# Windowed attention beside a binary FFN on one core: six visits a sequence in place of nine, 64-row scores in one pass, one rotation of seven PSUM banks

## The chip, the cores and the metric

The kernel runs on one core of a Trainium2 chip. The metric is the device time of one execution in microseconds (us), the lower the better. TensorE (PE in the profile) multiplies matrices and loads its weights (PEld), VectorE is DVE, ScalarE is ACT, GpSimd is POOL and SyncE is SP, which here issues nearly all DMAs. PSUM, where matmuls leave their results, is used here as eight banks; one bank holds 512 float32 numbers in each of 128 partitions.

## The reference

There are 8 sequences of 512 rows of 256 numbers. For each sequence, `x + attention(LN(x)) * silu(ffn(LN(x)))`:

```python
# attention: 16 heads of 16 numbers, q and k rotated (RoPE)
q, k, v = split(xn @ in_proj_w.T)
delta = pos[:, None] - pos[None, :]
mask = (delta >= 0) & (delta < 250)
scores = einsum('bhtd,bhsd->bhts', q, k) * 16 ** -0.5
attn = softmax(where(mask, scores, -huge))
s = einsum('bhts,bhsd->bhtd', attn, v) @ out_proj_w.T
# FFN: weights are +1 or -1, widths 512 (xn, -xn) -> 1024 -> 1024 -> 256
h = relu(s0 * [xn, -xn] @ W0) * 2;  h = relu(s1 * h @ W1) * 2;  h = s2 * h @ W2
out = x + s * silu(h)
```

## The kernel before, in words

Activations lie transposed: features in the partitions, the 512 positions of a sequence along the free dimension. Numbers that need float32 accuracy are held as two parts, high and low. In the FFN the high part is float16 and the low part fp32r. A tile of the second hidden layer (`layer`, "h2", 128 features) takes 16 matmuls of 512 columns; its bank is then read twice, by `high` (ACT, L535, relu) and by `low` (DVE, L533, what is left over). The third layer, `last` ("z"), takes 16 more. The first layer ("h1") takes 4 a tile.

**q and k.** `project` (L394) gives two halves of q and two of k; DVE multiplies them by cosines and sines (`times`, L410), POOL adds these up (`rotate`, L431), ACT copies out the high part (`split_hi`, L448: the tiles `kh` and `qh`) and DVE subtracts for the low part (`split_lo`, L455). `to_dram` writes high and low into DRAM, and `stack` (L458 to L464) loads them again, head by head: a head has 32 rows in the partitions, 16 of its high part and 16 of its low part, so four heads fill a tile. A score is k times q in full, that is high by high, low by low, high by low and low by high. With 32 rows that takes two matmuls that add up in PSUM ("turns"): k against q with its parts in order (`q0`), then against q with its parts exchanged (`q1`). Four heads are a group, and there are four groups.

**A visit.** Attention is cut into blocks: of a group g, the 128 keys j, and the queries that see them (378, 378, 256 and 128 for the four j). `steps` puts the 16 blocks, three of them cut in two, into nine visits a sequence of up to 512 columns a head. A visit (`step`, L860) first puts the score matmuls on PE (`scores`, L752), then the matmuls of the visit before with v (`values`, L826), then two ACT instructions of 2 banks each for the exponentials (`exponentials`, L771), then the masks on POOL (`mask`, L787 and L794: affine selects that put zeros outside the window). The sums over a row come out of the values matmul as an extra column. Between visits PE works on FFN layers and projections. After a group is done, `keep` copies V and the sums S out of the bank of `values` (even groups on ACT L850 and L851, odd groups on DVE L844 and L845).

**PSUM.** Before, three pools share the eight banks: `ps_s`, two tiles of two banks each, for scores; `ps_o`, one bank, for the values; `ps_m`, a rotation of three banks, for everything else (h, z, v, q, k and the output projection `att_ps`).

**The gate.** `z` is scaled (DVE, L616) and later turned into silu by `gate_ready`: exponential on ACT (L643), plus one on POOL (L647), two reciprocals of 256 columns on DVE (L652), and a product on POOL (L654). `project_o` (L959) multiplies attention by the output weights into a bank (`att_ps`); `product` (DVE, L981) multiplies bank and gate, and frees the bank; `store` adds x on POOL (L988) and writes out. This runs for two halves (u = 0 and 1) a sequence. The gate and output of sequence b are made late in sequence b+1, beside its last visits.

**Order.** Each engine works its instructions off in the order in which they were issued. That order comes from a small planner (`run`): a heap of pieces of work, each with a planned time (42 planner units a sequence) and a cost; a piece may return follow-ups with a delay (exponentials after scores, masks after exponentials). `attention` (L868) places the visits between FFN pieces. So an instruction that waits holds up whatever was put behind it on its engine.

The steps of the prediction touch `to_dram`, `stack`, `steps`, `scores`, `exponentials`, `mask`, `values`, `step`, `layer`, `gate_ready`, `project_o` and `divide`.

## Time and profile before

| what | value |
|---|---|
| median of 3 runs | 606.43 us (605.62 to 607.2) |
| the profiled execution | 605.76 us |
| its span, from the first to the last instruction | 603.9 us |
| outside the span | 1.86 us |
| PE busy | 593.9 us, 98% of the span |
| DVE, ACT, POOL busy | 337.3, 289.7 and 280.6 us |
| clock granted to PE | 1.00 |
| DMA | 75.52 MB, 125 GB/s on average |

Reading it: a group of instructions has its line, engine, operation and tiles, then its busy time and the mean of one; behind the bar stands the idle time of the engine just before these instructions, and what ended it. The chain that ended last is followed back from the last instruction. Busy time of PE includes pipelined matmuls, so 98% does not say that PE runs at its peak; it says that it seldom stands still. Where starts are compared below, they are of one kind of instruction, since modelled ends of matmuls overlap.

### The profile page before, as it was taken

Reading aid. Unit: us, or ns where it says so; the run is one execution under the profiler, and the core shown is the slowest. Engines: PE = TensorE matmul, PEld = TensorE weight load, DVE = VectorE, ACT = ScalarE, POOL = GpSimd, SP = SyncE. Lnnn points to the kernel's source line nnn. Section 1 sums busy time; section 2 is a strip of 40 time slices with the busy share of each in tenths; the row PEclk is TensorE's granted clock in tenths of the full one; section 3 lists DMA queues with packets and bytes.
Section 4 is the critical chain, followed back from the end, with each engine's and each line's share of the span. In section 5 each row is a group of like instructions: output and inputs, shape, how many; then the busy total and the mean of one; then the engine's idle time right before and its main releaser. Section 6 shows DMA issues by size and latency. Waiting matters only on the chain.

```text
span 603.9 us, 11263 instructions
## 1 busy us (share of the span) xinstructions
PE 593.9 (98%) x4492; PEld 366.7 (61%) x4492; DVE 337.3 (56%) x578; ACT 289.7 (48%) x411; POOL 280.6 (46%) x346
## 2 busy tenths in 40 slices
PE   7999999999999999999999999999999999999996
PEld 5654666555665556556566566655665556667785
DVE  6854535557456474655736656466565555635456
ACT  4755664444553535545354454543545425554432
POOL 2745522366423653437524456144662256436433
PEclk9999999999999999999999999999999999999999
DMA  8652642227331353415433254242442315322102
GB/s 269 235 177 88 231 144 90 87 82 237 108 125 53 133 186 107 126 53 203 118 107 125 82 198 131 88 130 99 174 163 88 109 71 210 112 56 71 58 15 64
DMA packets 43177, 75.52 MB, mean 125 GB/s; under 512 B 10224, under 2 KB 17904, under 8 KB 43120
## 3 DMA queue, kind: packets, MB, share of 16 engines
q1 hardware_dynamic: 40688, 72.53, 35.7%
q10 hardware_dynamic: 2432, 2.23, 1.2%
q8 instruction: 36, 0.59, 0.4%
q14 instruction: 21, 0.17, 0.1%
HBM read 44.83 MB, written 29.91 MB: 124 GB/s over the span
## 4 chain that ended last, share of the span: by engine, by line
PE 92%; DMA 3%; DVE 2%; POOL 1%; issue 0%; ACT 0%; ACTq 0%; SPq 0%; DVEq 0%
PE h_ps L524 46%; PE po L826 12%; PE z_ps L578 9%; PE sc L752 9%; PE v_ps L371 4%; PE att_ps L959 4%; PE ka_ps L394 2%; PE qa_ps L394 2%; PE kb_ps L394 2%; PE qb_ps L394 2%; DMA q<-dq 1%; DMA wqkv_sb<-in_w_qkv_dram 1%; DMA dq<-m_qa 1%; POOL m_qa L431 1%; POOL m_ka L431 0%
## 5 line engine op out<-in xcount | busy, mean ns | idle before, releaser
L771 ACT ACTIVATE p<-sc 128x1024 f32<-128x1024 f32 (+2 forms) x144 | 138.3, 1013 | 77.2 <-PE sc L752 46.8
L524 PE MATMUL h_ps<-h1l,w_sb 128*128 128x512 f32 (+1 forms) x576 | 146.1, 395 | 0.0
L787 POOL TENSOR_SCALAR_AFFINE_SELECT p<-p 128x512 f32<-128x512 f32 x128 | 93.7, 738 | 101.9 <-ACT p L771 101.1
L524 PE MATMUL h_ps<-h1h,w_sb 128*128 128x512 f16 (+1 forms) x576 | 123.1, 357 | 0.0
L524 PEld LDWEIGHTS h_ps<-h1l,w_sb 128*128 128x128 f32 x576 | 100.2, 188 | 29.5 <-issue 9.2
L524 PEld LDWEIGHTS <-w_sb 128*128 128x128 f16 x704 | 61.2, 98 | 74.7 <-issue 29.2
L535 ACT ACTIVATE h2h<-h_ps 128x512 f16<-128x512 f32 (+1 forms) x72 | 39.5, 548 | 124.5 <-PE h_ps L524 124.5
L794 POOL TENSOR_SCALAR_AFFINE_SELECT p<-p 128x512 f32<-128x512 f32 (+1 forms) x96 | 51.7, 539 | 87.7 <-ACT p L771 81.5
L826 PE MATMUL po<-p,v_pad 128*32 128x378 f32 (+4 forms) x1216 | 76.6, 372 | 0.0
L533 DVE SCALAR_TENSOR_TENSOR h2l<-h_ps,h2h 128x512 fp32r<-128x512 f32 (+1 forms) x72 | 44.0, 611 | 46.0 <-ACT h2h L535 45.9
L533 DVE SCALAR_TENSOR_TENSOR h1l<-h_ps,h1h 128x512 fp32r<-128x512 f32 x64 | 43.4, 688 | 42.2 <-ACT h1h L535 41.2
L652 DVE RECIPROCAL den<-den 128x256 f32<-128x256 f32 (+1 forms) x32 | 52.4, 1643 | 22.2 <-POOL den L647 22.2
L752 PEld LDWEIGHTS sc<-q,k 32*128 32x128 f32 x1216 | 44.2, 184 | 30.5 <-issue 22.5
L752 PE MATMUL sc<-q,k 32*128 32x378 f32 (+4 forms) x1216 | 58.0, 307 | 0.8 <-DMA q<-dq 0.8
L524 PE MATMUL h_ps<-xl,w_sb 128*128 128x512 f32 x128 | 52.3, 489 | 0.0
L826 PEld LDWEIGHTS po<-p,v_pad 128*32 128x32 f32 x1216 | 31.7, 109 | 28.4 <-issue 17.0
L535 ACT ACTIVATE h1h<-h_ps 128x512 f16<-128x512 f32 x64 | 38.1, 597 | 19.0 <-PE h_ps L524 19.0
L949 POOL TENSOR_TENSOR V<-V,R 128x512 f32<-128x512 f32 x16 | 20.6, 1286 | 46.3 <-DVE R L948 41.4
L524 PE MATMUL h_ps<-xh,w_sb 128*128 128x512 f16 x128 | 38.4, 382 | 0.1
L578 PE MATMUL z_ps<-h2l,w_sb 128*128 128x512 f32 (+1 forms) x144 | 35.7, 390 | 0.0
L431 POOL TENSOR_TENSOR m_ka<-m_ka,m_kb 128x512 f32<-128x512 f32 x16 | 20.1, 1274 | 31.7 <-DVE m_kb L410 31.7
L616 DVE TENSOR_SCALAR gate<-z_ps,scales 128x512 f32<-128x512 f32 (+1 forms) x16 | 11.5, 718 | 38.4 <-PE z_ps L578 38.4
(102 smaller groups left out, 679.1 us busy)
## 6 DMA issues: line engine op xcount, KB each, us to landing
q<-dq SPq DMA_DIRECT2D x64, 256.0 KB
dq<-qh SPq DMA_DIRECT2D x16, 512.0 KB
dq<-m_qa SPq DMA_DIRECT2D x16, 512.0 KB
k<-dk SPq DMA_DIRECT2D x32, 256.0 KB
dk<-kh SPq DMA_DIRECT2D x8, 512.0 KB
dk<-m_ka SPq DMA_DIRECT2D x8, 512.0 KB
x<-in_x_dram SPq DMA_DIRECT2D x30, 128.0 KB
xT<-in_x_t_dram SPq DMA_DIRECT2D x7, 512.0 KB
```

The lines of the kernel that those rows point to most:

```text
L394: nc.tensor.matmul(ps[:, cols], wqkv_sb[:, c, ds(col, P)], st["xT"][:, c, cols], start=(c == 0), stop=(c == EC - 1),)
L431: nc.gpsimd.tensor_tensor(m[:, i], m[:, i], n[:, i], op)
L524: nc.tensor.matmul(ph, weights(w, p, c, ts(f, P)), st[src + p][:, c, cols], start=(k == 0), stop=(k == n - 1),)
L533: nc.vector.scalar_tensor_tensor(lo, ph, 0.0, hi, ALU.max, ALU.subtract)
L535: high = lambda: nc.scalar.activation(hi, ph, AF.Relu)
L578: nc.tensor.matmul(pz, weights(w2, p, c, ts(f, P)), st["h2" + p][:, c, cols], start=(c == 0 and p == "h"), stop=(c == NF1 - 1 and p == "l"),)
L652: nc.vector.reciprocal(part, part)
L752: nc.tensor.matmul(sc[r // 2][:, r % 2, ds(off, n)], st["k0", g][row, ts(j, P)], st[f"q{turn}", g][row, ds(j * P + first, n)], start=(turn ...
L771: nc.scalar.activation(p[:, 2 * half : 2 * half + 2, :n], sc[half][:, :, :n], AF.Exp, scale=D ** -0.5,)
L787: nc.gpsimd.affine_select(out=block, in_=block, compare_op=ALU.is_ge, fill=0.0, base=0, pattern=[[0, 4], [1, P]], channel_multiplier=-1,)
L794: nc.gpsimd.affine_select(out=block, in_=block, compare_op=ALU.is_ge, fill=0.0, base=-1, pattern=[[0, 4], [-1, beyond]], channel_multiplier=1,
L826: nc.tensor.matmul(po[32 * r : 32 * r + 32, ds(j * P + first, n)], v_columns(j, g, r), p_[:, r, ds(off, n)], start=(j == 0), stop=(done an ...
```

## The change

The change does the same arithmetic with other shapes and another use of PSUM.

- A head's q and k get 64 rows: k as high, low, high, low and q as high, low, low, high. One matmul then holds all four products. A tile holds two heads, so a group has two pairs of tiles. Each of k's and q's parts is written to DRAM twice.
- Six visits a sequence (two blocks cut in two), each with up to 512 columns a head in four banks (x) and up to 256 in two more (y, two heads in a bank): up to 768 columns.
- All PSUM but the bank of `values` becomes one rotation of seven one-bank tiles (`ps_b`), from which scores, h, z, v, q, k and `att_ps` all take theirs.
- Exponentials are one instruction for each bank, six a visit; masks come in three parts, each behind two of the exponentials.
- Probabilities lie in tiles of two banks' width, eight in the pool. `S` and `R` share three buffers.
- The planner's cost of a visit is 2.5 in place of 1.7, and its exponentials may be issued up to 1.4 units before the values.

```diff
-    probs = ctx.enter_context(tc.tile_pool(name="probs", bufs=2))
+    probs = ctx.enter_context(tc.tile_pool(name="probs", bufs=8))
-    ps_s = ctx.enter_context(tc.tile_pool(name="ps_s", bufs=2, space=PSUM))
     ps_o = ctx.enter_context(tc.tile_pool(name="ps_o", bufs=1, space=PSUM))
-    ps_m = ctx.enter_context(tc.tile_pool(name="ps_m", bufs=3, space=PSUM))
+    ps_b = ctx.enter_context(tc.tile_pool(name="ps_b", bufs=7, space=PSUM))
+    def bank(name):
+        return ps_b.tile([P, T], F32, tag="b", name=name)
...
-            st["h"] = ps_m.tile([P, T], F32, tag="mm", name=f"h_ps_{b}_{f}")
+            st["h"] = bank(f"h_ps_{b}_{f}")
...
-        pp = ps_m.tile([P, T], F32, tag="mm", name=f"att_ps_{b}_{u}")
+        pp = bank(f"att_ps_{b}_{u}")
...
-        for turn in range(2 if what == "q" else 1):
-            if part == 0:
-                st["dram", what, turn] = dram.tile(
-                    [P, 4, T], F32, tag=f"{what}{turn}", name=f"d{what}{turn}_{b}"
-                )
+        if part == 0:
+            st["dram", what] = dram.tile([P, 8, T], F32, tag=what, name=f"d{what}_{b}")
+        for turn in range(2):
+            place = 2 * turn + (part ^ (turn if what == "q" else 0))
             nc.sync.dma_start(
-                st["dram", what, turn][:, ds(2 * (part ^ turn), 2), :], tile_.bitcast(F32)
+                st["dram", what][:, ds(2 * place, 2), :], tile_.bitcast(F32)
             )
...
-        for what in ("k0", "q0", "q1"):
-            t = stacks.tile([P, T], F32R, tag=what, name=f"{what}_{b}_{g}")
-            rows = st["dram", what[0], int(what[1])][32 * g : 32 * g + 32]
-            nc.sync.dma_start(t.bitcast(F32), rows.rearrange("p n t -> (p n) t"))
-            st[what, g] = t
+        for pair in range(2):
+            for what in "kq":
+                t = stacks.tile([P, T], F32R, tag=f"{what}{pair}", name=f"{what}_{b}_{g}_{pair}")
+                rows = st["dram", what][ds(32 * g + 16 * pair, 16)]
+                nc.sync.dma_start(t.bitcast(F32), rows.rearrange("p n t -> (p n) t"))
+                st[what, g, pair] = t
...
-            dp, dv = 1.5, 1.0
+            dp, dv = 1.5, 0.85
...
+    HALF_BANK = T // 2
+    steps = []
+    for g in range(0, NG, 2):
+        for of_x, of_y in (
+            ([(g, *whole_0), (g, *whole_3)], (g, *whole_2)),
+            ([(g, *whole_1), (g + 1, *whole_3)], (g + 1, *whole_2)),
+            ([(g + 1, *whole_0), (g + 1, *left_1)], (g + 1, *right_1)),
+        ):
+            blocks, off = [], 0
+            for block in of_x:
+                blocks.append((*block, 0, off))
+                off += block[3]
+            assert off <= T and of_y[3] <= HALF_BANK
+            steps.append(blocks + [(*of_y, 1, 0)])
...
     def scores(b, i):
         st = states[b]
+        sc = [bank(f"sc_{b}_{i}_{k}") for k in range(6)]
+        for y in range(2):
+            for pair in range(2):
+                for g, j, first, n, y_, off in steps[i]:
+                    if y_ != y:
+                        continue
+                    for r in range(2):
+                        row = slice(64 * r, 64 * r + 64)
+                        at = off + HALF_BANK * pair if y else off
+                        nc.tensor.matmul(
+                            sc[r + (4 if y else 2 * pair)][:, ds(at, n)],
+                            st["k", g, pair][row, ts(j, P)],
+                            st["q", g, pair][row, ds(j * P + first, n)],
+                            start=True,
+                            stop=True,
+                            skip_group_check=True,
+                        )
+        return sc
+
+    def exponentials(b, i, sc):
+        tiles = [
+            probs.tile([P, 2, T], F32, tag="p", name=f"p_{b}_{i}_{k}") for k in range(3)
         ]
+        n = sum(x[3] for x in steps[i] if not x[4])
+        n_y = steps[i][-1][3]
+
+        def of_bank(k):
+            p, s_ = tiles[k // 2][:, k % 2], sc[k]
+            if k < 4:
+                p, s_ = p[:, :n], s_[:, :n]
+            elif n_y < HALF_BANK:
+                p, s_ = (
+                    a.rearrange("p (u n) -> p u n", u=2)[:, :, :n_y] for a in (p, s_)
+                )
+            nc.scalar.activation(p, s_, AF.Exp, scale=D ** -0.5)
+            out = [(0.6, jobs[k + 1])] if k < 5 else []
+            if k % 2:
+                out.append((0.6, masks[k // 2]))
+            return out
...
-        S = st["S", g] = outs.tile([P, T], F32, tag=f"S{odd}", name=f"S_{b}_{g}", bufs=2)
+        S = st["S", g] = outs.tile([P, T], F32, tag="S", name=f"S_{b}_{g}", bufs=3)
...
-        return [(-0.7 if had else 0.0, exps)] + more
+        tiles, exps, rest = exponentials(b, i, sc)
+        pending.append((rest, (b, i, tiles)))
+        return [(-1.4 if had else 0.0, exps)] + more
...
-            out.append((times[n], 1.7, lambda n=n: step(b, n)))
+            out.append((times[n], 2.5, lambda n=n: step(b, n)))
...
-        R = outs.tile([P, T], F32, tag="R", name=f"R_{b}_{pair}")
+        R = outs.tile([P, T], F32, tag="S", name=f"R_{b}_{pair}", bufs=3)
```

More of the change, by code (lines that the diff above doesn't have):

```diff
@@ L331, in turn_x @@
                     st["x" + p] = one.tile([P, EC, T], dt, tag="x" + p, name=f"x{p}_{b}")
-        if not plain and t == 2:
-            pt = ps_o.tile([P, T], F32, tag="po", name=f"xnT_ps_{b}_{t}")
-            pt = pt[:, : EC * P].rearrange("p (c q) -> p c q", c=EC)
-        elif not plain and t < 2:
-            pt = ps_s.tile([P, 2, T], F32, tag="sc", name=f"xnT_ps_{b}_{t}")
-            pt = pt[:, 0, : EC * P].rearrange("p (c q) -> p c q", c=EC)
-        else:
-            pt = ps_m.tile([P, EC, P], F32, tag="mm", name=f"xnT_ps_{b}_{t}")
+        pt = bank(f"xnT_ps_{b}_{t}")[:, : EC * P].rearrange("p (c q) -> p c q", c=EC)
         for c in range(EC):
@@ L364, in project_v @@
         st = states[b]
-        if b == 0:
-            v = ps_s.tile([P, 2, T], F32, tag="sc", name=f"v_ps_{b}_{t}")[:, 0, :E]
-            v = v.rearrange("p (n s d) -> p n s d", s=2, d=D)
-        else:
-            v = ps_m.tile([P, H // 2, 2, D], F32, tag="mm", name=f"v_ps_{b}_{t}")
+        v = bank(f"v_ps_{b}_{t}")[:, :E].rearrange("p (n s d) -> p n s d", s=2, d=D)
         for c in range(EC):
@@ L384, in project @@
         col = E * "qk".index(what) + P * "ab".index(part)
-        if b == 0 and what == "q":
-            ps = ps_s.tile([P, 2, T], F32, tag="sc", name=f"{what}{part}_ps_{b}")[:, 0]
-        elif half == 1:
+        if half == 1:
             ps = st.pop(part)
         else:
-            ps = ps_m.tile([P, T], F32, tag="mm", name=f"{what}{part}_ps_{b}")
-            st[part] = ps
+            ps = st[part] = bank(f"{what}{part}_ps_{b}")
         for cols in [slice(0, T)] if half is None else [ts(half, T // 2)]:
@@ L562, in last @@
         f, cols = outputs(b)[u]
-        if how == "final":
-            pz = ps_s.tile([P, 2, T], F32, tag="sc", name=f"z_ps_{b}_{u}")[:, 0, : T // 2]
-        else:
-            pz = ps_m.tile([P, T], F32, tag="mm", name=f"z_ps_{b}_{u}")
-            if b + 1 == B:
-                pz = pz[:, : T // 2]
+        pz = bank(f"z_ps_{b}_{u}")
+        if b + 1 == B:
+            pz = pz[:, : T // 2]
         if how == "at once":
@@ L630, in plain_ffn @@
             for f in range(NF0):
-                ps = ps_m.tile([P, T], F32, tag="mm", name=f"f_h_{b}_{f}")
+                ps = bank(f"f_h_{b}_{f}")
                 for c in range(n):
@@ L721, in tile_attention_times_gated_ffn @@
     left_1, right_1 = (1, 0, cut), (1, cut, seen[1] - cut)
-    steps = [
-        [(0, *whole_0), (0, *left_1)],
-        [(0, *right_1), (0, *whole_2)],
-        [(0, *whole_3), (1, *whole_0)],
-        [(1, *whole_1), (1, *whole_3)],
-        [(1, *whole_2), (2, *whole_2)],
-        [(2, *whole_0), (2, *left_1)],
-        [(2, *right_1), (2, *whole_3), (3, *whole_3)],
-        [(3, *whole_0), (3, *left_1)],
-        [(3, *right_1), (3, *whole_2)],
-    ]
+    HALF_BANK = T // 2
[12 more added lines that the diff above has]
+            steps.append(blocks + [(*of_y, 1, 0)])
     used = [[n for n, step_ in enumerate(steps) if g in {x[0] for x in step_}] for g in range(NG)]
@@ L739, in once, with place @@
         return lambda: calls.pop()() if calls else None
+    def place(tiles, r, y, off, n):
+        if y:
+            return tiles[2][:, r % 2, ds(HALF_BANK * (r // 2) + off, n)]
+        return tiles[r // 2][:, r % 2, ds(off, n)]
     def scores(b, i):
         st = states[b]
-        sc = [
-            ps_s.tile([P, 2, T], F32, tag="sc", name=f"sc_{b}_{i}_{half}")
-            for half in range(2)
-        ]
-        off = 0
-        for g, j, first, n in steps[i]:
-            for turn in range(2):
-                for r in range(4):
-                    row = slice(32 * r, 32 * r + 32)
-                    nc.tensor.matmul(
-                        sc[r // 2][:, r % 2, ds(off, n)],
-                        st["k0", g][row, ts(j, P)],
-                        st[f"q{turn}", g][row, ds(j * P + first, n)],
-                        start=(turn == 0),
-                        stop=(turn == 1),
-                        skip_group_check=True,
-                    )
-            off += n
@@ L761, in scores @@
-        return sc, off
-    def exponentials(b, i, sc, n):
-        p = probs.tile([P, 4, T], F32, tag="p", name=f"p_{b}_{i}")
-        def exps():
-            half_of(0)
-            return [(0.3, second)]
-        def half_of(half):
-            nc.scalar.activation(
-                p[:, 2 * half : 2 * half + 2, :n], sc[half][:, :, :n], AF.Exp,
-                scale=D ** -0.5,
-            )
-        second = once(lambda: half_of(1) or [(0.6, masks)])
-        masks = once(lambda: mask(i, p))
-        return p, lambda: (second(), masks()), once(exps)
@@ L780, in mask @@
-    def mask(i, p):
-        off = 0
-        for g, j, first, n in steps[i]:
+        sc = [bank(f"sc_{b}_{i}_{k}") for k in range(6)]
[15 more added lines that the diff above has]
+                        )
@@ new lines, in scores @@
+        return sc
+    def exponentials(b, i, sc):
+        tiles = [
+            probs.tile([P, 2, T], F32, tag="p", name=f"p_{b}_{i}_{k}") for k in range(3)
+        ]
+        n = sum(x[3] for x in steps[i] if not x[4])
[13 more added lines that the diff above has]
+            return out
+        jobs = [once(lambda k=k: of_bank(k)) for k in range(6)]
+        masks = [once(lambda k=k: mask(i, tiles, k)) for k in range(3)]
+        return tiles, jobs[0], lambda: [f() for f in jobs + masks]
@@ L785, in mask @@
+    def mask(i, tiles, k):
+        p, heads = tiles[k], 2
+        if k == 2:
+            p, heads = p.rearrange("p a (u n) -> p (a u) n", u=2), 4
+        for g, j, first, n, y, off in steps[i]:
+            if y != k // 2:
+                continue
             if first == 0:
@@ L788, in mask @@
                     out=block, in_=block, compare_op=ALU.is_ge, fill=0.0,
-                    base=0, pattern=[[0, 4], [1, P]], channel_multiplier=-1,
+                    base=0, pattern=[[0, heads], [1, P]], channel_multiplier=-1,
                 )
@@ L795, in mask @@
                     out=block, in_=block, compare_op=ALU.is_ge,
-                    fill=0.0, base=-1, pattern=[[0, 4], [-1, beyond]],
+                    fill=0.0, base=-1, pattern=[[0, heads], [-1, beyond]],
                     channel_multiplier=1,
                 )
-            off += n
     def v_columns(j, g, r):
@@ L805, in tile_attention_times_gated_ffn, with values @@
     over = []
-    def values(b, i, p):
+    def values(b, i, tiles):
         st = states[b]
-        blocks, off = [], 0
-        for g, j, first, n in steps[i]:
-            blocks.append((g, j, first, n, p, off))
-            off += n
+        blocks = [(*x[:4], tiles, *x[4:]) for x in steps[i]]
         g = over[0][0] if over else blocks[0][0]
@@ L817, in values @@
         now.sort(key=lambda x: x[1:3] != (0, 0))
+        if not now:
+            return
         over[:] = [x for x in blocks if x[0] != g]
@@ L823, in values @@
         done = i >= used[g][-1]
-        for k, (_, j, first, n, p_, off) in enumerate(now):
+        for k, (_, j, first, n, tiles_, y, off) in enumerate(now):
             for r in range(4):
@@ L828, in values @@
                     v_columns(j, g, r),
-                    p_[:, r, ds(off, n)],
+                    place(tiles_, r, y, off, n),
                     start=(j == 0),
@@ L854, in flush @@
         if pending:
-            *before, of_step = pending.pop()
-            for f in before:
-                f()
+            before, of_step = pending.pop()
+            before()
             return values(*of_step)
     def step(b, i):
-        sc, n = scores(b, i)
+        sc = scores(b, i)
         had = len(pending)
         more = flush() or []
-        p, masks, exps = exponentials(b, i, sc, n)
-        pending.append((exps, masks, (b, i, p)))
-        return [(-0.7 if had else 0.0, exps)] + more
+        tiles, exps, rest = exponentials(b, i, sc)
+        pending.append((rest, (b, i, tiles)))
+        return [(-1.4 if had else 0.0, exps)] + more
     def attention(b, among):
@@ L1019, in add_up @@
     def add_up():
-        total = ps_m.tile([1, 3 * B], F32, tag="mm", name="total")
+        total = bank("total")[0:1, : 3 * B]
         nc.tensor.matmul(total, ones[:, 0:1], counts, start=True, stop=True)
@@ L1077, in shifted @@
         st = states[b]
-        row = slice(32 * r, 32 * r + 32)
+        row = slice(64 * (r % 2), 64 * (r % 2) + 64)
         j0 = max(0, t - 2)
@@ L1081, in shifted @@
         h = 4 * g + r
-        sc = ps_s.tile([P, 2, T], F32, tag="sc", name=f"f_sc_{b}_{t}_{h}")
-        for turn in range(2):
-            nc.tensor.matmul(
-                sc[:, 0, :n],
-                st[f"q{turn}", g][row, ts(t, P)],
-                st["k0", g][row, ds(j0 * P, n)],
-                start=(turn == 0),
-                stop=(turn == 1),
-            )
-        p = probs.tile([P, 4, WIN], F32, tag="p", name=f"f_p_{b}_{t}_{h}")
-        x_, e, eT = p[:, 0, :n], p[:, 1, :n], p[:, 2, :]
-        nc.scalar.copy(x_, sc[:, 0, :n])
+        sc = bank(f"f_sc_{b}_{t}_{h}")[:, :n]
+        nc.tensor.matmul(
+            sc,
+            st["q", g, r // 2][row, ts(t, P)],
+            st["k", g, r // 2][row, ds(j0 * P, n)],
+            start=True,
+            stop=True,
+        )
+        p, turned_ = (
+            probs.tile([P, 2, T], F32, tag="p", name=f"f_p{k}_{b}_{t}_{h}") for k in range(2)
+        )
+        x_, e, eT = p[:, 0, :n], p[:, 1, :n], turned_[:, 0, :WIN]
+        nc.scalar.copy(x_, sc)
         off = (t - j0) * P
@@ L1107, in shifted @@
         nc.scalar.activation(e, x_, AF.Exp, scale=D ** -0.5)
-        pt = ps_s.tile([P, 2, T], F32, tag="sc", name=f"f_pt_{b}_{t}_{h}")
+        pt = bank(f"f_pt_{b}_{t}_{h}")
         for j in range(n // P):
-            nc.tensor.transpose(pt[:, 0, ts(j, P)], e[:, ts(j, P)], ident)
-        nc.scalar.copy(eT[:, :n], pt[:, 0, :n])
+            nc.tensor.transpose(pt[:, ts(j, P)], e[:, ts(j, P)], ident)
+        nc.scalar.copy(eT[:, :n], pt[:, :n])
         for j in range(n // P):
```

## The prediction

> **What bounds the kernel now.** I read the page first, then the chain of waits in order of time for one steady sequence, then the timelines of DVE and POOL where the gate is made, then each engine's waits. The page:

> ```profile
> span 603.9 us, 11263 instructions
> ...
> PE 593.9 (98%) x4492; PEld 366.7 (61%) x4492; DVE 337.3 (56%) x578; ACT 289.7 (48%) x411; POOL 280.6 (46%) x346
> ...
> PE 92%; DMA 3%; DVE 2%; POOL 1%; issue 0%; ACT 0%; ACTq 0%; SPq 0%; DVEq 0%
> ...
> L771 ACT ACTIVATE p<-sc 128x1024 f32<-128x1024 f32 (+2 forms) x144 | 138.3, 1013 | 77.2 <-PE sc L752 46.8
> ...
> L652 DVE RECIPROCAL den<-den 128x256 f32<-128x256 f32 (+1 forms) x32 | 52.4, 1643 | 22.2 <-POOL den L647 22.2
> ```

> PE is the bound: it waits 4.5 us in all, outside the start hardly ever. So two things count: what PE does less, and whether it is made to wait. The chain through the late part of a sequence shows what a visit costs:

> ```profile
> 276.12 0.83 PE sc L752 x17
> 276.95 1.43 PE po L826 x24
> 278.38 3.68 PE h_ps L524 x16
> 282.06 0.73 PE sc L752 x16
> 282.79 0.77 PE po L826 x16
> 283.56 3.69 PE h_ps L524 x16
> 287.25 1.72 PE att_ps L959 x4
> ```

> No gap lies between these pieces: PE is fed throughout. The other engines run close behind. This is the gate on DVE, then on POOL:

> ```profile
> 211.35 1.75 DVE L652 RECIPROCAL den<-den 128x256 f32<-128x256 f32 x1 [1.99 <-POOL den L647]
> 213.02 0.63 DVE L533 SCALAR_TENSOR_TENSOR h2l<-h_ps,h2h 128x512 fp32r<-128x512 f32 x1
> 213.56 1.74 DVE L652 RECIPROCAL den<-den 128x256 f32<-128x256 f32 x1
> 215.22 0.63 DVE L533 SCALAR_TENSOR_TENSOR h2l<-h_ps,h2h 128x512 fp32r<-128x512 f32 x1
> 216.75 0.69 DVE L981 TENSOR_TENSOR gate<-att_ps,gate 128x512 f32<-128x512 f32 x1 [0.90 <-POOL gate L654]
> ...
> 225.75 0.69 DVE L981 TENSOR_TENSOR gate<-att_ps,gate 128x512 f32<-128x512 f32 x1 [1.50 <-POOL gate L654]
> ```

> ```profile
> 202.52 2.52 POOL L431 TENSOR_TENSOR m_qa<-m_qa,m_qb 128x512 f32<-128x512 f32 x2 [2.96 <-DVE m_qb L410]
> ...
> 209.82 1.49 POOL L647 TENSOR_SCALAR den<-den 128x512 f32<-128x512 f32 x1
> ...
> 215.44 1.27 POOL L654 TENSOR_TENSOR gate<-gate,den 128x512 f32<-128x512 f32 x1 [1.99 <-issue]
> 217.52 1.29 POOL L988 TENSOR_TENSOR gate<-gate,xr 128x512 f32<-128x512 f32 x1 [0.80 <-DVE gate L981]
> 218.77 1.49 POOL L647 TENSOR_SCALAR den<-den 128x512 f32<-128x512 f32 x1
> ```

> Here is the point on which this forecast turns. The h2 tile whose low part starts at 213.02 had its last matmul at 208.81 by the chain: its bank came free some 4.8 us late, because the low part stood behind a reciprocal, and that behind POOL. The bank of the first `att_ps` was done at 215.72 and freed at 217.44. PE did not feel it, since scores had banks of their own and the rotation of three could skip ahead. The changed kernel takes that cover away.

> **The change part by part.**

> *What PE saves.* The nine score rows of one sequence (226.60 to 299.84) sum to 6.50 us, the nine value rows to 8.95. Before, 19 blocks in two turns are 38 quads of concurrent matmuls. A quad of 378 columns starts the next after 157 ns, of 256 after 107; 244 and fewer stay at about 105, by the starts. That is 10 x 0.157 + 8 x 0.107 + 20 x 0.105 = 4.53 us, so 1.97 / 9 = 0.22 us a visit is fixed. Values are 4 x 4560 columns at 2.4 a ns (512 in 213 ns inside h), 7.60 us, so 1.35 / 9 = 0.15 is fixed. Entering a visit takes 0.11 more (318 to 327 ns between starts against 213 inside h). A visit thus costs 0.48 us before its columns; three fewer give 1.44. After, 18 blocks for two pairs are 36 steps of two matmuls: 12 x 0.157 + 8 x 0.107 + 16 x 0.105 = 4.42, if two 64-row matmuls run side by side as four 32-row ones do. That saves 0.11. In all 1.55 x 8 = 12.4 us. Ends: if pairs do not overlap, scores cost 4.4 us a sequence more, +35 us; nothing excludes a pair cheaper than 105 ns, -0.4 a sequence. I take the middle, since the quads' rows are the nearest.

> *ACT and POOL.* Exponentials go from 18 of about 1013 ns to 36 a sequence. A 512-column relu takes 597 ns, so 36 x 0.59 = 21.2 us against 18.2, +3 a sequence; back to back they start 0.49 apart. Masks go from 28 to 46 a sequence at the same number of columns; 512 columns take 0.63, 24 take 0.23, so a 256-column one takes about 0.40, and the 18 more cost about 3.6 us. Both engines were under half busy, so their sums cost nothing; their queues do, see below.

> [...]

> *DMA.* A sequence writes 8 x 512 KB in place of 6 and loads 16 x 256 KB in place of 12: 2 MB more, 5.3 us at the 373 to 391 GB/s of the start, all on SP's queue. In the steady part the average is 125 GB/s, and q is stacked many us ahead: 0. At the start it is not covered: the first scores wait for q, written at 26.15 (5.06 us) and loaded from 31.27 (3.76 us), while DMA is full from 26 to 30. The k parts, written twice, stand ahead of q on SP. One more MB of k is 2.7 us, one more load 0.7; ends 0 (SP's extra issues fall into idle stretches such as 18 to 20, 4 GB/s) and 3.4. I take 2.0, since part is idle time.

> *The shared S and R buffers, eight probability tiles.* Three S and R a pair of groups, one pair every half sequence: each is reused some 35 us later. 0. Ends -0.3 and +0.7 (an S copy) a pair.

> *One rotation of seven banks.* A visit takes six of the seven, so every bank freed late meets a score or the tile after it. In the instruction order of the changed kernel, the late visits read: visit 3, half h2, ka, half h2, kb, half h2, qa, qb, half h2, visit 4, h2_4, h2_5, att_0, visit 5, h2_6, half h2_7, att_1, half h2_7, visit 0 of the next sequence. The rotation gives visit 5's sixth score bank from h2_5, h2_6's bank from att_0, and the next visit 0's sixth from att_1. Time from the start of visit 3:

> PE: visits have 1140, 762 and 378 value columns: 0.48 + 0.74 + 1.90 = 3.12, 2.49 and 1.84 us. Five half h2 and four projections until visit 4: qb ends 15.35, visit 4 runs 17.18 to 19.67, h2_4 and h2_5 (3.65 each) end 26.97, att_0 (1.72) 28.69; visit 5 wants its sixth bank at 29.44.

> The other side: `times` of qb is done 1.6 later, 16.95; POOL rotates to 19.55; ACT copies `qh` to 20.65, and the last four exponentials of visit 4 stand behind it, to 22.65; their last masks to 24.1 or 24.2, and only then stands the gate's plus one on POOL. Then as in the rows: 1.53 to the first reciprocal (25.73); 1.67 to h2_4's low part, 0.54 to the second reciprocal, 1.67 to h2_5's low part, which ends at 30.25. PE waits 0.8. Then POOL's product starts 4.1 after the first reciprocal, 29.85, and `product` ends at 31.87, where visit 5 has ended at about 31.3: h2_6 waits 0.5. From this `product` (31.17) to the next: 0.77 to the store, 1.25, now the seven masks of visit 5 (2.87, in the rows there are three and they stand after the plus one), 1.52, 4.12, 1.32, 0.70: ends 43.7. From h2_6's start (31.87) PE needs 3.65 + 1.83 + 1.72 + 1.84 + 0.8 to the sixth bank of visit 0: 41.7. It waits 2.0.

> Together 3.3 to 3.5 us a sequence. One mask took 1.6 us beside DVE's `split_lo` (208.23 to 209.85), which would add up to 0.7: I take 3.5. Ends 2 (masks a little faster, a reciprocal less in the way) and 5. It meets the sequences that make a gate this late, 1 to 6: 21 us. In sequence 0, visit 3 takes its sixth bank from its own first and waits for that exponential, behind `kh` (1.05 on ACT): 0.8. In sequence 7 the gate is earlier: 0.5, ends 0 and 2.

> *Sum.* 605.8 (the profiled execution: span 603.9 and 1.9 around it) - 12.4 + 21 + 0.8 + 0.5 + 2.0 = 617.7. That execution is 0.7 below the median of the runs, so 618.4 for the median.

> **The rivals.**

> *Faster: the chain has slack.* Mechanism: the gate's chain ends before PE asks for the banks. It decides at 2 us: if the plus one at 24.2 were there at 22.2, and the masks of visit 5 did not stand ahead of the second, only the saving would be left: 605.8 - 12.4 + 3.3 + 0.7 = 597.4, range 594 to 603. For it: before, product to product took 9.0 us, under PE's 9.8. Against it: the seven masks now in between, and a wait that DVE shows already:

> ```profile
> DVE gate L981 <- POOL gate L654: 14.7, 12, 1.8
> ```

> Before, that wait was DVE's alone, 12 times; now a bank hangs on it.

> *Slower still.* Masks slowed beside DVE in every sequence, +1 us ahead of each plus one, make +2 a sequence, and head-of-line waits on ACT behind `qh` add to that: 630 to 645. For it: the 1.6 us mask. Against it: most masks took 0.59 to 0.63.

> *Pairs do not overlap.* +35 us: 653. Against it: quads of 32 rows did.

> *Stall and saving cancel.* 604.6 to 608.2, which is stalls of 1.2 to 1.8 a sequence (597.4 plus six of them): under my lower end of 2, unless the start is cheaper too.

> **How the numbers follow.** Forecast 0.61 (own range 610 to 630), faster 0.16, cancel 0.05, slower still 0.14, no overlap 0.04. A measurement of this kernel can tell about 0.3%, 1.8 us. Faster 0.16, same 0.05, slower 0.79. The range of 600 to 637 leaves out about a tenth at the lower end and a tenth at the upper.

> **What would show it.** Right: 576 score matmuls, 48 visits, PE waits named at `sc` and `h_ps` for DVE's L520 (low part) and its product, in total 15 to 30 us, longest about 2; score rows near 0.96 us and six a sequence; POOL's plus one straight behind masks. Wrong: PE waits under 6 us (the faster rival), or score rows near 1.7 (no overlap). [...] What would make the forecast wrong most simply is an error of 2 us in the chain from qb to the plus one.

## The result and the profile after

The changed kernel takes 647.50 us (median of 4, 639.10 to 648.76) against 606.22 us: a ratio of 1.0633, with a 95% interval of 1.053 to 1.0736. Forecast were 618.4 us and a range of 600 to 637: slower was right, the size was not; more than three times the forecast loss came. The ratio leaves out the run of 648.76 us, which is the profiled one and counts as slow because it lies over 1.5% above the fastest; a run of e10 that counts as fast has the same profile in all that is read here.

The profiled execution took 648.76 us, with a span of 647.0 us and a mean granted clock of 0.976. The page after, with the lines that answer to those of before and the group of the score matmuls:

```profile
span 647.0 us, 10374 instructions
...
PE 606.3 (94%) x3788; PEld 374.5 (58%) x3788; DVE 331.4 (51%) x578; ACT 293.1 (45%) x555; POOL 289.8 (45%) x490
...
L770 ACT ACTIVATE p<-sc 128x512 f32<-128x512 f32 (+2 forms) x288 | 149.2, 604 | 62.5 <-PE sc L745 61.9
...
L745 PE MATMUL sc<-q,k 64*128 64x378 f32 (+4 forms) x576 | 59.6, 319 | 20.4 <-DVE gate L981 10.3
L636 DVE RECIPROCAL den<-den 128x256 f32<-128x256 f32 (+1 forms) x32 | 52.6, 1645 | 45.8 <-POOL den L631 45.8
```

In the page before, the score matmuls hardly waited:

```profile
L752 PE MATMUL sc<-q,k 32*128 32x378 f32 (+4 forms) x1216 | 58.0, 307 | 0.8 <-DMA q<-dq 0.8
```

PE executes 704 instructions fewer and yet is busy 12 us longer. DVE, ACT and POOL change by 3 to 9 us, and fall in share. What is new stands in PE's waits:

```profile
PE sc L745 <- DVE gate L981: 10.3, 6, 1.7
PE h_ps L511 <- ACT p L770: 9.0, 6, 1.6
PE sc L745 <- DMA q<-dq: 7.4, 4, 2.7
...
PE h_ps L511 <- DVE gate L981: 2.0, 6, 0.3
PE sc L745 <- ACT p L770: 1.5, 1, 1.5
```

The first and fourth line are the forecast's own waits: banks of `att_ps`, which `product` (L981) frees late, six times each. The gate that holds them, on POOL and then on DVE, in the sequence that begins near 165 us:

```profile
227.01 0.22 POOL L797 TENSOR_SCALAR_AFFINE_SELECT p<-p 128x24 f32<-128x24 f32 x1
227.21 1.49 POOL L631 TENSOR_SCALAR den<-den 128x512 f32<-128x512 f32 x1
...
234.92 1.27 POOL L988 TENSOR_TENSOR gate<-gate,xr 128x512 f32<-128x512 f32 x1 [0.81 <-DVE gate L981]
...
238.30 0.64 POOL L797 TENSOR_SCALAR_AFFINE_SELECT p<-p 128x512 f32<-128x512 f32 x1
238.90 1.49 POOL L631 TENSOR_SCALAR den<-den 128x512 f32<-128x512 f32 x1
```

```profile
228.74 1.75 DVE L636 RECIPROCAL den<-den 128x256 f32<-128x256 f32 x1 [3.26 <-POOL den L631]
...
234.15 0.69 DVE L981 TENSOR_TENSOR gate<-att_ps,gate 128x512 f32<-128x512 f32 x1 [0.92 <-POOL gate L638]
...
245.82 0.69 DVE L981 TENSOR_TENSOR gate<-att_ps,gate 128x512 f32<-128x512 f32 x1 [1.44 <-POOL gate L638]
```

Both plus ones (L631) start right behind masks, as worked out. From one product to the next it is 11.67 us; before it was 9.00. And this is PE at the visit that needs the bank, in the timeline and then, in two windows of 3.4 us that follow one another, with the clock (the seventh number, after five engines' busy times):

```profile
243.91 0.95 PE L745 MATMUL sc<-q,k 64*128 64x378 f32 x9
246.56 0.65 PE L745 MATMUL sc<-q,k 64*128 64x256 f32 x3 [1.71 <-DVE gate L981]
247.14 3.18 PE L827 MATMUL po<-p,v_pad 128*32 128x378 f32 x32
```

```profile
core 0: us, PE busy (x) PEld busy (x) DVE busy (x) ACT busy (x) POOL busy (x), PEclk, DMA share, GB/s
243.30:246.70 3.40, 1.69 (x14) 1.08 (x14) 1.96 (x3) 2.54 (x5) 1.38 (x2) 1.00 0.00 0
246.70:250.10 3.40, 3.40 (x35) 1.79 (x39) 1.06 (x3) 0.00 (x0) 3.40 (x5) 0.51 0.28 88
```

Here is what the forecast did not have. PE stands for about half of the first window; in the next the granted clock is half (a half-clock stretch, from here on). The values matmuls of this visit, 1140 columns for each of four heads, take 3.5 us by their starts where an undisturbed visit takes 2.07. The clock records of the trace show nine such stretches inside the span, each 3.413 us long: three up to 94 us, then one behind each visit 0 of the six sequences with a late gate. Nine times half of 3.413 is 15.4 us, which is also (1 - 0.976) of 647. "PE busy" counts them as work. A second profile of the same kernel (e10, span 646.6 us) has the same nine.

The second wait, that of h2_2 (the third tile of h2) for an exponential, is at visit 3. This is DVE and then ACT there, one sequence later:

```profile
278.68 1.60 DVE L309 TENSOR_TENSOR xT<-xT,of_all 128x512 f32<-128x512 f32 x2 [2.18 <-DMA of_all<-d]
```

```profile
283.39 0.72 ACT L315 ACTIVATE xh<-xT,sgnx 128x512 f16<-128x512 f32 x1 [2.36 <-DVE xT L309]
284.02 0.58 ACT L522 ACTIVATE h2h<-h_ps 128x512 f16<-128x512 f32 x1
284.50 3.00 ACT L770 ACTIVATE p<-sc 128x506 f32<-128x506 f32 x6
```

The scores of visit 3 began at 280.23. Their exponentials stood behind `xh`, a step of the next sequence's layer norm, which waited for DVE's `xT`, and this for the wide load of mean and deviation (`of_all`). h2_2 takes the bank of the first score, so PE waited for ACT, ACT for DVE, DVE for a DMA. Before, the same row had the same wait, and no bank hung on it:

```profile
259.74 0.72 ACT L313 ACTIVATE xh<-xT,sgnx 128x512 f16<-128x512 f32 x1 [2.15 <-DVE xT L307]
260.37 0.58 ACT L535 ACTIVATE h2h<-h_ps 128x512 f16<-128x512 f32 x1
260.85 1.93 ACT L771 ACTIVATE p<-sc 128x1024 f32<-128x1024 f32 x2
```

### The profile page after: what moved, and what is told of

The parts are those of the page before. It is cut to its first block, busy times and chain, and to the rows that moved or that the text cites. A ratio compares the mean times of both kernels' runs of the same rounds, so it can differ in the third digit from the quotient of the medians.

```text
span 647.0 us, 10374 instructions
## 1 busy us (share of the span) xinstructions
PE 606.3 (94%) x3788; PEld 374.5 (58%) x3788; DVE 331.4 (51%) x578; ACT 293.1 (45%) x555; POOL 289.8 (45%) x490
## 2 busy tenths in 40 slices
DMA packets 50086, 92.24 MB, mean 143 GB/s; under 512 B 10992, under 2 KB 18672, under 8 KB 50032
## 5 line engine op out<-in xcount | busy, mean ns | idle before, releaser
L770 ACT ACTIVATE p<-sc 128x512 f32<-128x512 f32 (+2 forms) x288 | 149.2, 604 | 62.5 <-PE sc L745 61.9
L790 POOL TENSOR_SCALAR_AFFINE_SELECT p<-p 128x256 f32<-128x256 f32 (+1 forms) x224 | 100.3, 458 | 149.3 <-ACT p L770 144.7
L511 PE MATMUL h_ps<-h1h,w_sb 128*128 128x512 f16 (+1 forms) x576 | 124.6, 360 | 11.0 <-ACT p L770 9.0
L827 PE MATMUL po<-p,v_pad 128*32 128x378 f32 (+4 forms) x1152 | 83.0, 429 | 0.0
L745 PE MATMUL sc<-q,k 64*128 64x378 f32 (+4 forms) x576 | 59.6, 319 | 20.4 <-DVE gate L981 10.3
L745 PEld LDWEIGHTS sc<-q,k 64*128 64x128 f32 x576 | 45.9, 187 | 44.1 <-issue 23.0
L520 DVE SCALAR_TENSOR_TENSOR h1l<-h_ps,h1h 128x512 fp32r<-128x512 f32 x64 | 43.2, 688 | 48.3 <-ACT h1h L522 48.2
L520 DVE SCALAR_TENSOR_TENSOR h2l<-h_ps,h2h 128x512 fp32r<-128x512 f32 (+1 forms) x72 | 43.9, 611 | 44.5 <-ACT h2h L522 44.5
L797 POOL TENSOR_SCALAR_AFFINE_SELECT p<-p 128x256 f32<-128x256 f32 x144 | 59.9, 416 | 0.4 <-POOL p L790 0.4
L827 PEld LDWEIGHTS po<-p,v_pad 128*32 128x32 f32 x1152 | 35.4, 124 | 27.8 <-issue 20.4
L638 POOL TENSOR_TENSOR gate<-gate,den 128x512 f32<-128x512 f32 (+1 forms) x16 | 19.3, 1206 | 56.4 <-issue 29.0
```

The source lines that it names most:

```text
L511: nc.tensor.matmul(ph, weights(w, p, c, ts(f, P)), st[src + p][:, c, cols], start=(k == 0), stop=(k == n - 1),)
L520: nc.vector.scalar_tensor_tensor(lo, ph, 0.0, hi, ALU.max, ALU.subtract)
L745: nc.tensor.matmul(sc[r + (4 if y else 2 * pair)][:, ds(at, n)], st["k", g, pair][row, ts(j, P)], st["q", g, pair][row, ds(j * P + first, n)],
L770: nc.scalar.activation(p, s_, AF.Exp, scale=D ** -0.5)
L790: nc.gpsimd.affine_select(out=block, in_=block, compare_op=ALU.is_ge, fill=0.0, base=0, pattern=[[0, heads], [1, P]], channel_multiplier=-1,)
L797: nc.gpsimd.affine_select(out=block, in_=block, compare_op=ALU.is_ge, fill=0.0, base=-1, pattern=[[0, heads], [-1, beyond]], channel_multi ...
```

## The experiments

The theory after the result: the late banks cost about what was forecast; the rest is the clock behind the waits, visit 3's bank, and the loads at the start. The first four kernels tell these apart. All times are medians; ratios are against the kernel before on the same chip.

### e1: free the bank of att_ps at once

```diff
+            def copied():
+                nc.scalar.copy(att, pp)
+                return [(0.0, product)]
...
-            nc.vector.tensor_tensor(y, pp, y, ALU.mult)
+            nc.vector.tensor_tensor(y, att if b + 1 < B else pp, y, ALU.mult)
```

> The changed kernel, with one more ACT copy of each att_ps (512 columns, about 0.6 us) out of PSUM, so that its bank no longer waits for the gate. Theory (two causes in one place): the wait of visit 0 for the product (2.05 us a sequence) and of h2_6 (0.41) go, six times each, -15 us; and because the half clock that follows the 2 us wait goes with it (1.7 us a sequence), another -10 us: about 622 us, and the value row of visit 0 falls from 3.5-3.7 to 2.07 us. Rival A (the long value row of visit 0 is a cost of the layout, for instance of banks read by other engines, and not of the wait): -15 us alone, about 632, value row still 3.5. Rival B (the next late bank takes over, h2_5's low part or the exponentials): under -8 us, a new wait of 1.5 to 2 us named at sc or h_ps.

Measured: 623.51 us (ratio 1.0279, 1.0233 to 1.0326), 24 us less than the changed kernel, though ACT does 14 copies more. The spans of the profiled executions differ by 25.1 us: 14.8 are the two waits (6 x (2.05 + 0.41)), 10.2 six half-clock stretches. The value row of visit 0 in the sequences with a late gate is 2.07 us again, the only half-clock stretches left inside the work are the three of the start, and both waits for L981 are gone:

```profile
PE h_ps L511 <- ACT p L770: 9.4, 6, 1.6
PE sc L745 <- DMA q<-dq: 7.4, 4, 2.6
...
PE sc L745 <- DVE h2l L520: 0.3, 2, 0.2
```

Two effects in one place, as the theory had it; rival A's 632 and rival B's new wait did not come. But h2_5's low part, which the forecast had holding visit 5 by 0.8 us, is hardly in this list: visit 5's score row stays at 1.3 us against 1.0 elsewhere.

### e2: fill the wait with idle work

```diff
+        for _ in range(7 if b > 0 and i == 0 else 0):
+            nc.tensor.matmul(
+                sc[0], st["k", 0, 0][:, 0:P], st["q", 0, 0], start=True, stop=True,
+                skip_group_check=True,
+            )
```

> The changed kernel with seven idle matmuls of 512 columns (1.5 us at full clock) ahead of the scores of visit 0 in sequences 1 to 7; their result is overwritten. Nothing waits less for it. Theory (the clock halves after a window in which PE mostly stands still): the wait of visit 0 shrinks from 2.05 to about 0.6 us, no half clock follows it in sequences 2 to 7, and the kernel gets faster by 6 x 1.7 = 10 us though PE does more: about 637 us against 647.5. Rival (the long value row has another cause): no gain, 647 to 650, value row still 3.5 us.

Measured: 634.85 us (1.048, 1.0434 to 1.0525). PE does 49 matmuls more and the kernel is 12.7 us faster, though the bank comes no earlier: the row of scores of visit 0 still takes 3.2 us, filler included (3.1 to 3.4 in the changed kernel, where the longer ones end at half clock). But the clock stays, here in the stretch before and in that with the values of a visit 0:

```profile
309.00:312.40 3.40, 3.40 (x13) 1.84 (x12) 2.09 (x2) 0.14 (x1) 1.28 (x1) 1.00 0.08 28
312.40:315.80 3.40, 3.40 (x20) 2.55 (x20) 1.94 (x3) 0.60 (x1) 1.29 (x1) 1.00 0.00 0
```

In that execution one half-clock stretch is left inside the work, at 38.3 us, in place of nine. From one visit 0 to the next, a steady sequence takes 76.85 us on average in place of 78.56 (sequences 2 to 7 of the profiled executions): 1.70 us less, about half of 3.413, and the start has no part in it. The clock is a cause of its own, not a cost of the layout. The gain is above the expected 10 us, since two of the three stretches at the start are gone too: one behind visit 0 of sequence 1, where the filler also stands, and one behind visit 3 of sequence 0, where nothing was filled (1.48 us without a matmul in its window, as in the changed kernel, where half clock did follow; see the last section).

### e3: layer norm of the next sequence earlier

```diff
-            at = dict(load=9, stats=9, down=10.5, over=12, ...
+            at = dict(load=9, stats=7.0, down=8.7, over=10.0, ...
```

> The changed kernel with the layer norm statistics of the next sequence planned 2 units earlier (stats 7.0 for 9, down 8.7 for 10.5, over 10.0 for 12), so that the wide load of mean and deviation lands some 3 to 4 us earlier and ACT is not held by xh when visit 3 comes. Theory: h2_2's wait for the first exponential of visit 3 (1.55 us a sequence) goes, and most of the 0.1 to 0.9 us of visit 3's sixth score bank: -9 to -13 us, 634.5 to 638.5, if the half clock stays as it is. Rival (ACT is late at visit 3 by its own load of six exponentials): under -3 us.

Measured: 627.10 us (1.0353, 1.0308 to 1.0399), 20 us less, where 9 to 13 were expected. The wait of h2_2 for ACT is gone from PE's list; that of visit 0 for L981 stands unchanged, six times:

```profile
PE sc L745 <- DVE gate L981: 10.4, 6, 1.8
...
PE h_ps L511 <- DVE gate L981: 2.0, 6, 0.3
```

The spans differ by 24.4 us (the profiled execution is the fastest of its four): 12 are visit 3's wait and its score bank, the rest is the clock again, with two half-clock stretches in place of nine (11.9). Of the six waits of visit 0 only two (near 160 and 235 us) were still followed by one, and none at the start. Why the others were not is the subject of the last section.

### e4: 64 rows and one pass alone

```diff
-            for turn in range(2):
-                for r in range(4):
-                    row = slice(32 * r, 32 * r + 32)
+            for pair in range(2):
+                for r in range(2):
+                    row = slice(64 * r, 64 * r + 64)
                     nc.tensor.matmul(
-                        sc[r // 2][:, r % 2, ds(off, n)],
-                        st["k0", g][row, ts(j, P)],
-                        st[f"q{turn}", g][row, ds(j * P + first, n)],
+                        sc[pair][:, r, ds(off, n)],
+                        st["k", g, pair][row, ts(j, P)],
+                        st["q", g, pair][row, ds(j * P + first, n)],
```

with `to_dram` and `stack` as changed; nine visits and the PSUM pools of before.

> The kernel before with one part of the change alone: 64 rows a head, one pass, k and q each written twice; still nine visits, two-bank exponentials and the PSUM pools of before. Theory: two 64-row matmuls overlap, scores cost the same, the price is the start alone (k's second write ahead of q): +1 to +4 us, 607 to 610. Rival: pairs do not overlap as quads do, 36 to 38 score steps of twice the length, +20 to +35 us.

Measured: 614.97 us (1.0134, 1.0095 to 1.0173). The nine score rows of a steady sequence sum to 6.46 us against 6.51 in the same sequence before: two 64-row matmuls overlap as four 32-row ones do, and the rival falls. But the layout's price is 8.4 us, all of it in the first 85 us (a steady sequence takes 73.3 us, as before), where the forecast had 2.0:

```profile
PE sc L752 <- DMA q<-dq: 6.0, 4, 2.2
```

Of these, the first visit has 3.3 us (0.5 before) and the visit that begins group 3 of sequence 0 has 2.6 (0.2 before), and half clock follows both: for two windows of 3.413 us from 36.5 us on, and for one from 74.0.

### e5: the gate earlier, by its planned time alone

```diff
-            out.append((late(b, u) - 4.5, 0, lambda: gate_ready(b, u)))
+            out.append((late(b, u) - (9.0 if u == 0 else 5.5), 0, lambda: gate_ready(b, u)))
```

> The changed kernel with the planned time of the gate moved (9.0 units ahead of its projection in place of 4.5 for u = 0, 5.5 for u = 1). It adds and removes no instruction; on POOL the first plus one now stands ahead of the rotation of k, the second ahead of the masks of visit 5, and on DVE no reciprocal stands ahead of h2_4's and h2_5's low parts. Theory (the gate's place in the queues of POOL and DVE holds the banks): the waits of visit 5, h2_6 and visit 0 go as with the copy of att_ps, and the half clock with them: 620 to 626 us. Rival (it is POOL's load, not the order): the wait moves to q's rotation or to the masks, 635 or more, with a wait at sc or po for POOL or ACT.

Measured: 626.77 us (1.0328, 1.03 to 1.0356). Without one instruction more or less, 21 us go: it is the gate's place in the queues, not the load of POOL. Visit 5's score row falls from 1.3 to 0.99 us, so its 0.3 was the gate's too: the reciprocals no longer stand ahead of the low parts. Some of it moves:

```profile
PE sc L745 <- ACT p L770: 3.2, 7, 1.5
```

Six of these seven times are new: the score row of each visit 4 takes 1.68 us in place of 1.00, for an exponential that stands behind `qh`, which stands behind the later rotation of q.

### e6: the copy and the earlier layer norm together

> The copy of att_ps by ACT and the earlier layer norm statistics together, the start left as it is. Theory (separate causes that add up): PE waits in the steady sequences are nearly all gone; left are the start (q's loads, 3.8 us, and 4.2 us at sequence 1), visit 3 of sequence 0 (1.9) and the half clocks after them (about 5): 606.2 - 12.4 + 15 = 608.5, between 605 and 612. Rival (taking away two waits uncovers a third, as large): over 614, with a new wait in the steady sequences.

Measured: 611.05 us (1.0068, 1.0044 to 1.0093). The causes add up in the spans: 14.8 for the banks of `att_ps`, 12 for visit 3 and 10.2 for six half-clock stretches make 37.0, and the span is 36.5 us shorter than the changed kernel's. The gains of e1 and e3 do not add up (24 and 20), since each had taken half clock behind visit 0 with it. In the steady sequences visit 5's 0.3 us is left; the rest lies before 95 us: q's loads 4.2 us, one wait of 2.1 at a load, visit 3 of sequence 0 1.5, and three half-clock stretches.

### e7 and e8: the start in another order

```diff
-        for pair in range(2):
-            for what in "kq":
+        for what in "kq":
+            for pair in range(2):
...
-        first, end = SEQ * b + (20.6 if b == 0 else 0.0), ends_at(b)
+        first, end = SEQ * b + (22.4 if b == 0 else 0.0), ends_at(b)
...
-                3.5 if b == 0 else 4.0 if b == 1 else 9.0
+                5.3 if b == 0 else 8 if b == 1 else 9.0
```

e7 has this with the copy and the earlier layer norm, e8 with the gate's earlier planned time in place of the copy.

> As the run before, and the start mended by order alone: the first visit of sequence 0 one h2 tile later, the loads of k ahead of those of q, and the first stack of sequence 1 ahead of the inverse sums on SP's queue. Theory: the first wait falls from 3.8 to under 1 us, the one at sequence 1 from 4.2 to under 1, visit 3 of sequence 0 under 1, with their half clocks: 596 to 602 us, faster than the kernel before by about 1%. Rival (the loads are bound by DMA, not by their place in the queue): 604 to 609.

> The same mended start and the earlier statistics, with the gate's earlier planned time in place of the copy of att_ps: the changed kernel with planned times and the order of two loops alone altered, no instruction added. Theory: as the run before without its 14 copies, which were off PE's path: 596 to 602 us, within 1 us of it. Rival (the rotation of k and q, now behind a plus one on POOL, delays the scores of the next sequence): slower than the run before by 3 us or more.

Measured: e7 604.93 us (0.998, 0.9969 to 0.9992), e8 609.27 us (1.0052, 1.0035 to 1.0069). The waits for q's loads are gone in both, and DMA still moves 92.24 MB: they were a matter of order, that of the loads on SP's queue and the place of the first visit, which were not tried one by one. But e7 missed its 596 to 602, for one new wait, the first line here (the second stands in every trace):

```profile
PE ka_ps L381 <- ACT p L770: 3.8, 1, 3.8
PE warm L232 <- POOL ident masks.py:199: 2.8, 1, 2.8
```

With its visits placed later, sequence 0 met visit 3's trouble at its visit 1: the exponentials stood behind `xh`, and ka takes one of their banks. Half clock follows, for two windows. e8's rival held: it is 4.3 us slower than e7, with 0.7 us in each visit 4 (behind q's rotation and `qh`) against 0.3 in e7's visits 5, and 2.7 us in two visits of the last sequence, whose gates moved too.

### e9: the wide load of sequence 1 earlier

```diff
-                at.update(load=18.65, stats=15, down=18, over=18.7, norm=24.8, ...
+                at.update(load=17.16, stats=15, down=17.12, over=17.2, norm=25.4, ...
...
+            elif g == 1:
+                at += 0.04
```

> As e7 (copy of att_ps, earlier statistics, mended start), and in sequence 0 SP's queue writes the moments of sequence 1 between the loads of the first two groups, so that the wide load of mean and deviation comes some 3 us earlier and ACT's exponentials of visit 1 are not held by xh. Theory: the wait of ka for that exponential (3.8 us) and the half clock behind it (1.7) go: 604.9 - 5.5 = 599.5, between 598 and 602, faster than the kernel before by about 1%. Rival (the loads of the second group, now later, hold visit 1): 603 to 606, with a wait at sc for q's load.

Measured: 602.42 us (0.9936, 0.9923 to 0.995): faster than the kernel before by 0.64%, just above the expected 598 to 602. The wait of ka fell from 3.8 to 1.2 us and 0.7 for `xT`, and one half-clock stretch at 49.6 us stayed:

```profile
PE ka_ps L381 <- ACT p L770: 1.2, 1, 1.2
PE ka_ps L381 <- DVE xT L309: 0.7, 1, 0.7
```

A steady sequence takes 72.4 us here and in e7, against 73.25 before: 0.85 us less.

### e10: the changed kernel again

> The changed kernel once more, unaltered, to see how its time spreads. Theory (half-clock windows of fixed length fall on a grid of their own; a wait of 2 us halves the clock only where enough of it lies in one window): executions differ by how many of the six waits of visit 0 are followed by a half window, in steps of about 1.7 us each: between 637 and 649, more spread than the kernel before (605 to 608), and the granted clock goes with the time (0.976 at 647, 0.99 at 638). Rival (the spread is of another kind): the clock in the records does not follow the time.

Measured: 647.69 us (1.0675, 1.0643 to 1.0707), from 643.93 to 649.43, and the clock goes with the time. Over the eight executions of the changed kernel, span times (1 - clock) is what the clock took. For four of them: 647.6 us at 0.976, 645.2 at 0.979, 642.2 at 0.981 and 637.4 at 0.989 lose 15.5, 13.5, 12.2 and 7.0, and leave 632.1, 631.7, 630.0 and 630.4. The other four, all at 0.976, leave 629.2 to 631.5. The spread of 10 us is for the most part the clock; without it 3 remain over the eight.

## Why the prediction was right and wrong

The span grew by 43.1 us. By the prediction's own terms, with waits taken from the starts of matmuls in the trace (h2_2's from the list of waits):

| term | forecast | measured | from |
|---|---|---|---|
| three visits fewer | -12.4 | about -9.5 | e7, e9: 0.85 a sequence, and 0.33 of visit 5's wait is still in it: 1.18 x 8 |
| late banks in sequences 1 to 6 | +21 | +16.6 | 6 x (0.3 visit 5, 0.41 h2_6, 2.05 visit 0) |
| visit 3 in sequences 1 to 6 | 0 | +12 | 6 x (1.50 h2_2, 0.49 sixth score bank) |
| start and sequence 0 | +2.8 | +8.9 | first visit 3.0 more than before, visit 3 1.9, first visit of sequence 1 4.0 more |
| sequence 7 | +0.5 | +0.4 | visit 2's scores |
| half clock | 0 | +15.4 | 9 x 3.413 / 2 |
| sum | +11.9 | +43.8 | |

**The late banks: right, in place, cause and size.** The two banks of `att_ps` and their order of magnitude came as worked out from the rows: 2.0 forecast and 2.05 measured at visit 0, 0.5 and 0.41 at h2_6. e1 and e5 take them away, once by freeing the bank and once by order. Too large was visit 5 (0.8; 0.3 measured). e1 shows visit 5's 0.3 to stay when the products are out of the way, and e5 shows it to go with the reciprocals. (The text counts five half tiles of h2 from visit 3 to visit 4, where its own order lists four; its 17.18 us fits four, and e3, where nothing waits there, has 17.19.)

**The half clock: the step that failed most.** The forecast's sum has no term for the clock, and 15.4 us came: nine stretches of 3.413 us in the clock records, at half clock. The waits of 2.05 us at visit 0 were enough for it: in the window of 3.413 us ahead of each of the six stretches behind visit 0, PE stood for about half of the time (1.59 to 1.73 us without a matmul). e2 is the proof: more work (49 matmuls), less time (12.7 us).

**Visit 3: missed.** "One rotation of seven banks" followed the banks of visit 5, h2_6 and visit 0, looked at visit 3 in sequence 0 alone (0.8), and stopped there. h2_2 takes the bank of visit 3's own first score, so it waits for ACT to reach that exponential. The row was in sight before: there too, `xh` waited 2.15 us for DVE and the exponentials came behind it. The step that failed is that these waits were put at nothing in sequences 1 to 6; 12 us came, and e3 takes them away.

**The start: mis-sized.** The forecast had one wait for q, with 2.0 us, and visit 3 of sequence 0, with 0.8. The first took 3.0, the second 1.9, and the first visit of sequence 1, which the forecast did not have, 4.0. e7 removes both waits for q by order, without a byte less of DMA; visit 3's falls to 0.7. The later loads of sequence 1 stood behind an inverse that waited for its sums.

**The saving: a fifth to a quarter too large.** The 0.48 us a visit counted the entry into a visit against 213 ns between matmuls inside a tile; without the visit there is a change of tile in its place, which takes about 235: some 0.07 us a sequence. And each score row is 0.99 to 1.01 us, not 0.96: some 0.24 a sequence. Together that is most of what is missing.

**ACT's and POOL's loads, DMA in the steady part, S and R: right at nothing.** ACT is 45% busy with 288 exponentials. Not the load of emptying PSUM bound here, but when a bank was emptied: 16.6 us for the late banks and 12 at visit 3.

The rivals: "faster" needed 2 us of slack at each bank. It is what e9 reaches with other means, and gives 602.4 where 597.4 were reckoned. Pairs overlap, by e4. "Slower still" (630 to 645) came nearest in time, for reasons that do not carry it: with masks slowed beside DVE the products would stand further apart than reckoned (11.83 us), and they stand 11.67 apart; the wait behind ACT's queue that did come stood behind `xh`, not `qh`.

## What to carry to other kernels

When several users of PSUM are put into one rotation, go through every bank of it, not only those with a known late reader: here visit 0 and h2_2 inherited the lateness of the instruction that read their bank's last tenant, and of all that stood before that on its engine (10.3 us in six waits of visit 0 for the gate, 9.0 in six of h2_2 for the exponential behind `xh`). A wait of 2.05 us at visit 0 cost some 3.7 in all, with the 1.7 of the half-clock stretch behind it; so look at the granted clock beside the waits, and at busy time that grows while instructions fall. Where such waits are a matter of order, planned times are the cheap cure (e5: 21 us without an instruction).

## What the hardware showed that was not expected

**The steady sequences kept step with the grid.** From one visit 0 to the next, the steady sequences of the changed kernel take 78.56 us on average (78.35 to 78.87), and 23 windows are 78.51: the wait falls into nearly the same place of a window each time, and each is followed by half clock. In e3 a sequence takes 76.6 us with a half-clock stretch and 74.9 without, 22.4 and 21.9 windows; there the wait slid along the grid, and after two half-clock stretches the next four waits were cut in two by a grid point (1.54 us or less in one window) and went free. That is why 20 us came from a change worth 12. Nothing here shows that the grid holds the period at 23 windows: e2's 76.85 us and half a window make 78.56 as well, so the step may be an accident of this length, and no run altered the length alone. That executions of one kernel differ by where their waits meet the grid fits the clock of e10 and was not seen directly: both traces of the changed kernel have all nine stretches.
